# An AdaLN attention and mixture-of-experts layer on one core: where the zero rows are written, and how the first block's q, k and v are made

## The chip, the cores and the metric

The kernel runs on one core of a Trainium2 chip. The metric is the device time of one execution in microseconds, median of the runs. A core has five engines that run side by side, each its own list of instructions in order: TensorE (PE; its weight loads are PEld), VectorE (DVE), ScalarE (ACT), GpSimd (POOL) and SyncE (SP). Here SP issues nearly all transfers, ACT some, and POOL the indirect ones. Sixteen DMA engines carry out what the queues issue. [...]

## The reference

One layer of a diffusion transformer on x of shape 4 x 2048 x 256 in float32: a modulated LayerNorm, causal attention with 16 heads of size 16 and rotary positions, a gated residual, a second modulated LayerNorm, and a mixture of 16 experts (4 chosen of each token) with a shared expert. Cut to what matters here:

```python
mod = (silu(c) @ wmod).reshape(4, 6, 1, 256)
sa, ca, ga, sb, cb, gb = six parts of mod
h = layernorm(x) * (1 + ca) + sa
q, k, v = split(h @ qkv_w + qkv_b)            # 16 heads of 16
q, k = rotary(q), rotary(k)
attn = softmax(mask(q @ k.T / 4)) @ v
x = x + ga * (attn @ out_w + out_b)
h = layernorm(x) * (1 + cb) + sb
tidx, tw = route(h)                           # 4 of 16 experts for a token
y = sum over the chosen experts of tw * (silu(h @ w1.T) * (h @ w3.T)) @ w2.T
x = x + gb * (y + shared expert(h))
```

## The kernel before

**Blocks.** The 8192 tokens are 16 blocks of 512 (`BT`), four to a batch row; a block is four tiles of 128 tokens. The kernel has a start (constants and the modulation), an attention part (up to about 2430 us in the profile) and an expert part.

**The start.** Constants are loaded through SP. Then a pool named `zero` is opened: DVE fills a tile `zeros` of 128 x 2 x 272 (L203, L204; the four columns that name experts get -1), and ACT issues 32 writes of it (L207), one for each of 16 experts in each of two phases, to the DRAM arrays `xs`. They set the first 256 rows of each expert's region. Tokens are scattered into `xs` later by POOL (L489), and those rows stand in front of an expert's own. The pool is closed, and the pools of the modulation are opened in the memory that it gave back: `wm` (1.5 MB, L233), `sg` (L235), the matmuls on them (L240, L253), two gates on DVE, and a write of the result to DRAM (`rowd`, L265). When these are closed in turn, the attention's constants (`wqkv`, `bqkv`, `rp` and others) go into memory that they used.

**A prologue for each block** (`prologue`): load x (`xb`, L657), normalise on DVE and POOL, transpose with PE (L303), scale and shift on ACT into `hT` (L664). Then, for each tile `t` in turn: q and k as one matmul group of 512 columns into a PSUM tile `pq` (L698), bias on DVE (`qk`, L702); v into `pv` (L711), bias on DVE into `va` (L714); two products with the rotary table on POOL (L725) and their sum on POOL (L734); four transpositions of 128 x 128 into `ptq` (L739); and on ACT a copy rounded to the matmul's short float32 form (`high`, L748) and an exact copy (`whole`, L750). POOL subtracts one from the other (`low`, L678, function `lower`). `pq`, `pv`, `ptq` and the transposed x all share the one buffer of PSUM pool `wps`, so each waits until the one before has been read.

`high` and `low` hold two tiles and have one buffer. After the second and the fourth tile `store` writes them to DRAM (`qd`, `kd`) in 16 transfers of 8 heads x 16 x 256 (L689), 128 KB each; the third tile's `high` must wait until these have been read. v goes to `vd` (L756). The stores are for the next stage, in which a unit loads its heads (`load`): `qt` (L775), `kt` (L782) and `vg` (L785), with three buffers each.

**Units.** A unit is one group of four heads of one block of the first batch row, or of two blocks of a later one. `row_max` computes scores (L803, L826) only to find the row maxima on DVE (L813, L836); then the scores are computed again with the maxima subtracted (L1055, L1062), exponentiated on ACT (L1070), masked on POOL (L1074) and multiplied with v (L1003). The maxima of the next unit are found between the steps of the current one. PSUM pool `psp` has three buffers of two banks for scores, `pop` one bank for sums.

**Order.** Within the attention and expert parts PE, ACT, DVE and POOL run in the order in which the code is written. The transfers on SP are put in order by a planner. Before the first unit the code drains `prologue(0)` and the first unit's maxima; all other prologues, the ends of blocks and the routing are generators, pulled in pieces between the steps of the units. A piece states its need (a bank, DVE time, POOL time) and takes it from a `Budget` that each step refills, which can run into debt; due times (`due`) force a prologue's pieces in any case. `PIECES` is the number of pieces that `prologue(0)` had, and sets the due times.

Of the kernel before, what the change touches and what calls it, by code (L numbers as in the profile page):

```python
# [8 lines left out]
F32 = mybir.dt.float32  # L9
FR = mybir.dt.float32r  # L10
# [4 lines left out]
ALU = mybir.AluOpType  # L15
AX = mybir.AxisListType

P = 128
B, T, D = 4, 2048, 256
H, HD = 16, 16  # L20
NG = 4
BT = 512
HB = BT // 2
NQ = T // BT
NB = B * NQ
E, I = 16, 192
EW = 2 * 2 * I + 2 * D
N = B * T
TT = 256
TC = TT // P  # L30
# [5 lines left out]
ROW = D + 4 + 4 + 8  # L36
# [84 lines left out]
def adaln_attention_moe(  # L121
# [17 lines left out]
    nc = tc.nc  # L139
# [3 lines left out]
    const = ctx.enter_context(tc.tile_pool(name="const", bufs=1))  # L143
# [3 lines left out]
    ident = const.tile([P, P], F32, name="ident")  # L147
# [29 lines left out]
    phases = [Phase(blocks) for blocks in PHASES]  # L177
# [20 lines left out]
    nc.gpsimd.iota(  # L198
        four, [[4 * P, 4]], base=-1, channel_multiplier=4, allow_small_or_imprecise_dtypes=True
    )  # L200
    with tc.tile_pool(name="zero", bufs=1) as zp:
        zeros = zp.tile([P, TC, ROW], F32, name="zeros")
        nc.vector.memset(zeros, 0.0)  # L203
        nc.vector.memset(zeros[:, :, D : D + 4], -1.0)  # L204
        for ph in phases:
            for e in range(E):
                nc.scalar.dma_start(  # L207
                    ph.xs[e * ph.region : e * ph.region + TT, :].rearrange(
                        "(p t) d -> p (t d)", p=P
                    ),  # L210
                    zeros.rearrange("p t d -> p (t d)"),
                )

    mod = const.tile([P, 4, B], F32, name="mod")
# [12 lines left out]
    with tc.tile_pool(name="modw", bufs=1) as mw, tc.tile_pool(  # L229
        name="modp", bufs=1, space=PSUM  # L230
# [7 lines left out]
        for m in range(4):  # L238
            for k in range(2):
                nc.tensor.matmul(  # L240
                    pm[:, m, :],
                    lhsT=wm[:, k, m * P : (m + 1) * P],
                    rhs=sg[:, k, :],
                    start=(k == 0),
                    stop=(k == 1),
# [4 lines left out]
        for m in range(4):  # L250
            pr = mp.tile([B, D], F32, name=f"pr{m}")
            for k in range(2):
                nc.tensor.matmul(  # L253
                    pr,
                    lhsT=sg[:, k, :],
                    rhs=wm[:, k, (2 + m) * D : (3 + m) * D],
                    start=(k == 0),
                    stop=(k == 1),
# [336 lines left out]
    vd = [dram.tile([P, NG, 4, VG], F32, name=f"vd{n}") for n in range(NB)]  # L595

    with ExitStack() as actx:
# [3 lines left out]
        tp = actx.enter_context(tc.tile_pool(name="ta", bufs=2))  # L601
        ep = actx.enter_context(tc.tile_pool(name="ea", bufs=4))

        psp = actx.enter_context(tc.tile_pool(name="ps", bufs=3, space=PSUM))
        pop = actx.enter_context(tc.tile_pool(name="po", bufs=1, space=PSUM))
        wps = actx.enter_context(tc.tile_pool(name="wps", bufs=1, space=PSUM))
# [15 lines left out]
        wqkv = acst.tile([P, 2, 3 * D], F32, name="wqkv")  # L622
        nc.sync.dma_start(wqkv, qkv_w.rearrange("(k p) n -> p k n", p=P))
        bqkv = acst.tile([P, 3 * D], F32, name="bqkv")
# [5 lines left out]
        rp = acst.tile([P, T // P, 2, 2, HD // 2], F32, name="rp")  # L630
# [15 lines left out]
        va_new = acst.tile([P, NG, 4, VG], F32, name="va")  # L646
        vh = va_new[:, :, :, : 4 * (HD + 1)].rearrange("p g t (h e) -> p g t h e", e=HD + 1)
# [4 lines left out]
        def prologue(n):  # L652

            b, qb = divmod(n, NQ)
            yield 0, 0, 0
            xb = xp.tile([P, 4, D], F32, tag="xp", name="xb")
            nc.sync.dma_start(xb, x[n * BT : (n + 1) * BT, :].rearrange("(t p) d -> p t d", p=P))  # L657
            for _ in range(3):
                yield 0, 0, 0
            xn = yield from normalise(xb, tp, xb)  # L660
            yield 1, 0, 0

            def evict(to, pt, k):
                nc.scalar.activation(  # L664
                    to,
                    pt,
                    AF.Identity,
                    bias=mod[:, k, b : b + 1],
                    scale=mod[:, 2 + k, b : b + 1],
                )  # L670

            hT = yield from transposed(xn, "hT", tp, wps, "w", evict)


            rest = None

            def lower(cols, whole, high, low):
                nc.gpsimd.tensor_tensor(  # L678
                    low[:, :, cols], whole, high[:, :, cols].bitcast(F32), ALU.subtract
                )  # L680

            def store(half, high, low):

                for c_ in range(4):
                    to = (qd, kd)[c_ // 2][n].rearrange("(h part d) t -> part h d t", part=4, d=HD)
                    to = to[:, 8 * (c_ % 2) : 8 * (c_ % 2) + 8]
                    for part in range(4):
                        of = (high, low, *((high, low) if c_ < 2 else (low, high)))[part]
                        nc.sync.dma_start(  # L689
                            to[part][:, :, half * HB : (half + 1) * HB], of[:, c_, :].bitcast(F32)  # L690
                        )

            for t in range(4):
                lT = [hT[:, k, t * P : (t + 1) * P] for k in range(2)]
                yield 1, 0.7, 0
                pq = wps.tile([P, BT], F32, tag="w", name="pq")
                for k in range(2):
                    nc.tensor.matmul(  # L698
                        pq, lhsT=lT[k], rhs=wqkv[:, k, : 2 * D], start=(k == 0), stop=(k == 1)
                    )  # L700
                qk = tp.tile([P, 2 * D], F32, tag="qk", name="qk", bufs=1)
                nc.vector.tensor_add(qk, pq, bqkv[:, : 2 * D])  # L702
                yield 0, 0, 1.3 if rest is not None else 0
                if rest is not None:
                    lower(*rest)
                    if t == 2:
                        store(0, *rest[2:])
                yield 1, 0.4, 0
                pv = wps.tile([P, D], F32, tag="w", name="pv")
                for k in range(2):  # L710
                    nc.tensor.matmul(  # L711
                        pv, lhsT=lT[k], rhs=wqkv[:, k, 2 * D :], start=(k == 0), stop=(k == 1)
                    )
                nc.vector.tensor_add(  # L714
                    vh[:, :, t, :, 1:],
                    pv.rearrange("p (g h e) -> p g h e", g=NG, e=HD),
                    bqkv[:, 2 * D :].rearrange("p (g h e) -> p g h e", g=NG, e=HD),
                )
                parts = qk.rearrange("p (h e two) -> p h e two", e=HD // 2, two=2)
                full = [P, 2 * H, 2, HD // 2]  # L720
                prod = []
                for s in range(2):
                    yield 0, 0, 1.3
                    r_ = tp.tile(full, F32, tag=f"r{s}", name=f"r{s}", bufs=1)
                    nc.gpsimd.tensor_tensor(  # L725
                        r_,
                        parts[:, :, :, s].unsqueeze(2).to_broadcast(full),
                        rp[:, qb * 4 + t, s].unsqueeze(1).to_broadcast(full),
                        ALU.mult,
                    )  # L730
                    prod.append(r_.rearrange("p h a e -> p h (a e)"))
                xr = prod[0]
                yield 0, 0, 1.3
                nc.gpsimd.tensor_tensor(xr, xr, prod[1], ALU.add)  # L734
                yield 0, 0, 0
                yield 1, 0, 0
                pt = wps.tile([P, 4, P], F32, tag="w", name="ptq")
                for c_ in range(4):
                    nc.tensor.transpose(  # L739
                        pt[:, c_, :],  # L740
                        xr[:, 8 * c_ : 8 * c_ + 8, :].rearrange("p h d -> p (h d)"),
                        ident,
                    )
                if t % 2 == 0:
                    high = tp.tile([P, 4, HB], FR, tag="high", name="high", bufs=1)
                    low = tp.tile([P, 4, HB], FR, tag="low", name="low", bufs=1)
                cols = slice(t % 2 * P, (t % 2 + 1) * P)
                nc.scalar.copy(high[:, :, cols], pt)  # L748
                whole = tp.tile([P, 4, P], F32, tag="whole", name="whole", bufs=1)
                nc.scalar.copy(whole, pt)  # L750
                rest = (cols, whole, high, low)
            yield 0, 0, 1.3
            lower(*rest)
            yield 0, 0, 0
            store(1, *rest[2:])
            nc.sync.dma_start(vd[n], va_new)  # L756

        qts, kts, vas = {}, {}, {}


# [196 lines left out]
        ahead, maxes, after_max, over, ends, after = (Background(budget) for _ in range(6))  # L957
        ahead.add(prologue(0))
        ahead.drain()
        PIECES = ahead.pulled  # L960
        ahead.pulled = 0
        load(0)
        load(1)
        maxes.add(row_max(*units[0][0]))
        maxes.drain()
        after_max.drain()
        for n in range(1, NQ):
            ahead.add(prologue(n))
        for n in range(NQ, NB, NQ):
# [49 lines left out]
        for u, unit in enumerate(units):  # L1019
# [22 lines left out]
            for s_, (n, g, k_, nkt, off) in enumerate(steps_):  # L1042
# [9 lines left out]
                for q in range(2):  # L1052
                    for h_ in range(2):
# [3 lines left out]
                            start=True, stop=False,  # L1057
                        )
                for q in range(2):
                    for h_ in range(2):  # L1060
# [3 lines left out]
                            lhsT=kt[rows, q, k_ * P : (k_ + 1) * P],  # L1064
# [437 lines left out]
```

## Time and profile before

| | us |
|---|---|
| median of 3 runs | 3942.05 (3936.0 to 3945.19) |
| the profiled execution's own time | 3947.4 |
| its span | 3945.6 |
| `zeros` written, first issue to last landing | 1.84 to 31.7 |
| `wm` issued; first matmul on it | 31.68; 38.50 |
| `hT` of block 0 complete | 64.3 |
| first score matmul | 129.66 |
| first scatter into `xs` | 572.7 |
| PE, DVE, ACT, POOL busy | 3315.9, 2583.1, 1525.7, 1531.1 |

Times within an execution count from the start of its span. The span runs from the first instruction to the last; the execution's own time is 1.8 us more. The clock in a window's row is the granted clock of TensorE as a share of the full one, and the DMA share is the mean busy share of the sixteen DMA engines.

### The profile page before, as it was taken

How to read it: one execution, taken by the hardware profiler on the slowest of the kernel's cores; microseconds unless marked ns; L12 is line 12 of the kernel's file. 1: busy time of each engine (PE TensorE's matmuls, PEld its weight loads, DVE VectorE, ACT ScalarE, POOL GpSimd, SP SyncE). 2: the span in 40 equal slices, each digit the busy share in tenths (PEclk: the TensorE clock that was granted, in tenths of full speed). 3: DMA queues.
4: the chain of work that ended last, by engine and by line, in shares of the span. 5: the costliest groups of instructions: out<-in, count | busy, mean ns of one | idle time of the engine just before them, and what ended most of it. 6: DMA issues, size and time to landing. Idle time of an engine off the chain costs nothing. (4 is left out here: it accounts for less than half of the span.)

```text
span 3945.6 us, 56494 instructions
## 1 busy us (share of the span) xinstructions
PE 3315.9 (84%) x20276; PEld 1727.9 (44%) x20400; DVE 2583.1 (65%) x4644; ACT 1525.7 (39%) x2188; POOL 1531.1 (39%) x2222
## 2 busy tenths in 40 slices
PE   3567888888888989988898888899788889899994
PEld 1223333333334433333433333343377677676662
DVE  1344676767776777767767776677276576667775
ACT  0223344544444544544454454455522222222220
POOL 1223243352434342343425334310146556545555
PEclk7668898988999988988999998899999899899997
DMA  4233233341223322233332222220177567678763
GB/s 168 91 101 115 84 128 112 121 147 54 85 96 125 116 94 91 82 108 117 108 110 100 83 99 81 96 73 28 59 272 243 199 231 250 217 270 303 275 252 139
DMA packets 275115, 544.96 MB, mean 138 GB/s; under 512 B 27534, under 2 KB 143246, under 8 KB 274834
## 3 DMA queue, kind: packets, MB, share of 16 engines
q1 hardware_dynamic: 242578, 454.79, 33.9%
q0 software_dynamic: 27648, 77.63, 5.3%
q10 hardware_dynamic: 4608, 8.91, 0.6%
q8 instruction: 161, 2.64, 0.3%
q14 instruction: 120, 0.98, 0.1%
HBM read 351.42 MB, written 189.81 MB: 137 GB/s over the span
## 5 line engine op out<-in xcount | busy, mean ns | idle before, releaser
L1070 ACT ACTIVATE e<-st 128x1024 f32<-128x1024 f32 (+3 forms) x1280 | 1078.8, 895 | 1039.5 <-PE st L1062 960.3
L813 DVE TENSOR_REDUCE mparts<-ps 128x2 f32<-128x1024 f32 (+3 forms) x1152 | 1180.0, 1044 | 457.1 <-PE ps L803 409.4
L803 PE MATMUL ps<-kt,qt 64*128 64x512 f32 (+3 forms) x3328 | 613.6, 414 | 177.9 <-ACT e L1070 66.7
L1003 PE MATMUL po<-e,vg 128*32 128x512 f32 (+3 forms) x5120 | 670.6, 590 | 29.5 <-POOL e L1074 14.8
L803 PEld LDWEIGHTS ps<-kt,qt 64*128 64x128 f32 x3328 | 303.3, 203 | 769.3 <-ACT e L1070 447.3
L1074 POOL TENSOR_SCALAR_AFFINE_SELECT e<-e 128x256 f32<-128x256 f32 x512 | 204.7, 410 | 952.2 <-ACT e L1070 948.1
L1171 PE MATMUL gu<-xT,wt 128*128 128x256 f32 x1920 | 465.4, 397 | 24.1 <-issue 11.4
L1274 POOL DMA_INDIRECT yd<-yt,to x320 | 315.8, 987 | 390.7 <-ACT hb L1182 208.3
L1062 PE MATMUL st<-qt,kt 64*128 64x512 f32 (+3 forms) x2560 | 462.3, 441 | 0.0
L1171 PEld LDWEIGHTS gu<-xT,wt 128*128 128x128 f32 x1920 | 371.3, 198 | 112.9 <-issue 45.5
L1055 PE MATMUL st<-mt,pick 32*128 32x512 bf16 (+3 forms) x2560 | 302.5, 373 | 79.7 <-DVE mparts L813 49.0
L489 POOL DMA_INDIRECT xs<-row,rowx x256 | 248.4, 970 | 177.7 <-DVE row L480 122.7
L836 DVE TENSOR_REDUCE mparts<-ps 128x8 f32<-128x1024 f32 x128 | 156.7, 1224 | 196.8 <-PE ps L803 181.8
L1062 PEld LDWEIGHTS st<-qt,kt 64*128 64x128 f32 x2560 | 206.2, 199 | 138.5 <-issue 126.7
L725 POOL TENSOR_TENSOR r<-qk,rp 128x512 f32<-128x512 f32 x128 | 164.8, 1306 | 189.3 <-DVE qk L702 185.7
L1270 ACT ACTIVATE yt<-y,of 128x256 f32<-128x256 f32 x160 | 67.1, 470 | 403.5 <-DVE is L1250 213.9
L1055 PEld LDWEIGHTS <-pick 32*128 32x128 bf16 x2560 | 87.4, 92 | 303.2 <-issue 291.1
L1003 PEld LDWEIGHTS po<-e,vg 128*32 128x32 f32 x5120 | 109.2, 112 | 186.9 <-issue 129.1
L678 POOL TENSOR_TENSOR low<-whole,high 128x512 fp32r<-128x512 f32 x64 | 81.4, 1271 | 253.7 <-ACT whole L750 253.7
L1209 PE MATMUL y<-wt,ha 128*128 128x256 f32 x640 | 158.6, 389 | 10.8 <-issue 7.7
L698 PE MATMUL pq<-wqkv,hT 128*128 128x512 f32 x256 | 145.1, 694 | 17.4 <-ACT whole L750 14.9
L1209 PEld LDWEIGHTS y<-wt,ha 128*128 128x128 f32 x640 | 118.6, 195 | 32.7 <-issue 14.7
(209 smaller groups left out, 3603.4 us busy)
## 6 DMA issues: line engine op xcount, KB each, us to landing
wt<-in_w_all SPq DMA_DIRECT2D x160, 640.0 KB
kt<-kd SPq DMA_DIRECT2D x124, 512.0 KB
xt<-xs SPq DMA_DIRECT2D x160, 272.0 KB
qt<-qd SPq DMA_DIRECT2D x64, 512.0 KB
yg<-yd SPq DMA_DIRECT2D x16, 2048.0 KB
vg<-vd SPq DMA_DIRECT2D x124, 168.0 KB
xb<-in_x SPq DMA_DIRECT2D x32, 512.0 KB
qd<-high SPq DMA_DIRECT2D x128, 128.0 KB
```

The costliest lines, as they stand in the source:

```text
L489: s_ = nc.gpsimd.indirect_dma_start(out=ph.xs[:, :], out_offset=bass.IndirectOffsetOnAxis(ap=rowx[:, n, t, j : j + 1], axis=0), in_=row[:, ...
L725: nc.gpsimd.tensor_tensor(r_, parts[:, :, :, s].unsqueeze(2).to_broadcast(full), rp[:, qb * 4 + t, s].unsqueeze(1).to_broadcast(full), ALU ...
L803: nc.tensor.matmul(ps[:, half, to : to + width], lhsT=qt[rows, q, t * P : (t + 1) * P], rhs=kt[rows, q, key : key + width], start=start, s ...
L813: nc.vector.tensor_reduce(to, ps[:, :, :width], AX.X, ALU.max)
L1003: nc.tensor.matmul(po[32 * j : 32 * j + 32, off:], lhsT=va[:, k_, j * (HD + 1) : j * (HD + 1) + 32], rhs=es[j // 2][:, j % 2, off:], start ...
L1055: nc.tensor.matmul(sts[q][:, h_, off:], lhsT=pick[rows, :], rhs=mt[rows, off:], start=True, stop=False,)
L1062: nc.tensor.matmul(sts[q][:, h_, off:], lhsT=kt[rows, q, k_ * P : (k_ + 1) * P], rhs=qt[rows, q, off:], start=False, stop=True,)
L1070: nc.scalar.activation(es[q][:, :, off:], sts[q][:, :, off:], AF.Exp, scale=SCALE)
L1074: nc.gpsimd.affine_select(out=es[q][:, :, off : off + P], in_=es[q][:, :, off : off + P], compare_op=ALU.is_ge, fill=0.0, base=0, pattern= ...
L1171: nc.tensor.matmul(ps[:, c_ * TT : (c_ + 1) * TT], lhsT=wt[:, c_, k * 2 * I + cols : k * 2 * I + cols + P], rhs=xT[:, k, c_ * TT : (c_ + 1 ...
L1209: nc.tensor.matmul(pss[half][:, t, :], lhsT=ha[:, at_ : at_ + P], rhs=wt[:, half, 4 * I : 4 * I + D], start=(t == 0), stop=False, skip_gro ...
L1274: s_ = nc.gpsimd.indirect_dma_start(out=ph.yd[:, :], out_offset=bass.IndirectOffsetOnAxis(ap=to[:, t : t + 1], axis=0), in_=yt[:, t, :], i ...
```

## The change

The zeros become a tile of 128 x 272 in the constants' memory. They are filled by POOL after the code of the first unit's maxima, and written from SP, with each row of the tile written twice:

```diff
-    with tc.tile_pool(name="zero", bufs=1) as zp:
-        zeros = zp.tile([P, TC, ROW], F32, name="zeros")
-        nc.vector.memset(zeros, 0.0)
-        nc.vector.memset(zeros[:, :, D : D + 4], -1.0)
-        for ph in phases:
-            for e in range(E):
-                nc.scalar.dma_start(
...
+    zeros = const.tile([P, ROW], F32, name="zeros")
...
         maxes.drain()
         after_max.drain()
+        nc.gpsimd.memset(zeros, 0.0)
+        nc.gpsimd.memset(zeros[:, D : D + 4], -1.0)
+        for ph in phases:
+            for e in range(E):
+                nc.sync.dma_start(
+                    ph.xs[e * ph.region : e * ph.region + TT, :].rearrange(
+                        "(p t) d -> p t d", p=P
+                    ),
+                    zeros.unsqueeze(1).to_broadcast([P, TC, ROW]),
+                )
```

Block 0 gets a function of its own, `opening`, instead of the loop over tiles. q, k and v of a tile go into one two-bank buffer of the score pool `psp`, which has three; the biased q and k go into buffers of the pool `ep` that the units use for exponentials. Of the two rotary products one is made on POOL and one on DVE, and the sum on DVE. Copies into `high` and `whole` are in a function `high_low`, which both paths use.

```diff
+            def opening(hT, high_low, store):
+                full = [P, 2 * H, 2, HD // 2]
+                qks, rots = {}, {}
+                def project(t):
+                    ps = psp.tile([P, 2, BT], F32, tag="s", name="first")
+                    for to, cols in ((ps[:, 0], slice(0, 2 * D)), (ps[:, 1, :D], slice(2 * D, 3 * D))):
+                        for k in range(2):
+                            nc.tensor.matmul(to, lhsT=hT[:, k, t * P : (t + 1) * P], rhs=wqkv[:, k, cols],
...
+                    qk = ep.tile([P, 2, BT], F32, tag="e", name="qk0")
+                    nc.vector.tensor_add(qk[:, 0], ps[:, 0], bqkv[:, : 2 * D])
+                    nc.vector.tensor_add(vh[:, :, t, :, 1:], ...
+                def rotate(t):
...
+                    for s, eng in enumerate((nc.gpsimd, nc.vector)):
+                        r_ = tp.tile(full, F32, tag=f"r{s}", name=f"r{s}", bufs=1)
+                        eng.tensor_tensor(r_, ..., ALU.mult)
...
+                    nc.vector.tensor_add(xr, prod[0], prod[1])
+                def split(t):
...
+                    cols, whole = high_low(t, pt)
+                    high, low = parts_[0]
+                    lower(cols, whole, high, low)
+                    if t % 2:
+                        store(t // 2, high, low)
+                project(0)
+                project(1)
+                rotate(0)
+                project(2)
+                for t in range(4):
+                    if t < 3:
+                        rotate(t + 1)
+                    if t == 0:
+                        project(3)
+                    split(t)
```

Block 0's stores go out on two queues, and its prologue ends after `opening`; `PIECES` becomes the number that it was before:

```diff
-                        nc.sync.dma_start(
+                        queue = nc.scalar if n == 0 and part % 2 else nc.sync
+                        queue.dma_start(
...
+            if n == 0:
+                opening(hT, high_low, store)
+                nc.sync.dma_start(vd[n], va_new)
+                return
...
+        PIECES = 48
...
         ahead.add(prologue(0))
         ahead.drain()
-        PIECES = ahead.pulled
```

More of the change, by code (lines that the diff above doesn't have):

```diff
@@ L200, in adaln_attention_moe @@
     )
-    with tc.tile_pool(name="zero", bufs=1) as zp:
-        zeros = zp.tile([P, TC, ROW], F32, name="zeros")
-        nc.vector.memset(zeros, 0.0)
-        nc.vector.memset(zeros[:, :, D : D + 4], -1.0)
-        for ph in phases:
-            for e in range(E):
[L207 to L212, printed above, removed]
+    zeros = const.tile([P, ROW], F32, name="zeros")
     mod = const.tile([P, 4, B], F32, name="mod")
@@ L675, in prologue, with high_low @@
             rest = None
+            parts_ = [None]
+            def high_low(t, pt):
+                if t % 2 == 0:
+                    parts_[0] = tuple(
+                        tp.tile([P, 4, HB], FR, tag=name, name=name, bufs=1)
+                        for name in ("high", "low")
+                    )
+                cols = slice(t % 2 * P, (t % 2 + 1) * P)
+                nc.scalar.copy(parts_[0][0][:, :, cols], pt)
+                whole = tp.tile([P, 4, P], F32, tag="whole", name="whole", bufs=1)
+                nc.scalar.copy(whole, pt)
+                return cols, whole
@@ new lines, in opening @@
+            def opening(hT, high_low, store):
[5 more added lines that the diff above has]
+                        for k in range(2):
+                            nc.tensor.matmul(
+                                to,
+                                lhsT=hT[:, k, t * P : (t + 1) * P],
+                                rhs=wqkv[:, k, cols],
+                                start=(k == 0),
+                                stop=(k == 1),
+                            )
+                    qk = ep.tile([P, 2, BT], F32, tag="e", name="qk0")
+                    nc.vector.tensor_add(qk[:, 0], ps[:, 0], bqkv[:, : 2 * D])
+                    nc.vector.tensor_add(
+                        vh[:, :, t, :, 1:],
+                        ps[:, 1, :D].rearrange("p (g h e) -> p g h e", g=NG, e=HD),
+                        bqkv[:, 2 * D :].rearrange("p (g h e) -> p g h e", g=NG, e=HD),
+                    )
+                    qks[t] = qk
+                def rotate(t):
+                    qk = qks.pop(t)
+                    parts = qk[:, 0].rearrange("p (h e two) -> p h e two", e=HD // 2, two=2)
+                    prod = []
+                    for s, eng in enumerate((nc.gpsimd, nc.vector)):
+                        r_ = tp.tile(full, F32, tag=f"r{s}", name=f"r{s}", bufs=1)
+                        eng.tensor_tensor(
+                            r_,
+                            parts[:, :, :, s].unsqueeze(2).to_broadcast(full),
+                            rp[:, t, s].unsqueeze(1).to_broadcast(full),
+                            ALU.mult,
+                        )
+                        prod.append(r_.rearrange("p h a e -> p h (a e)"))
+                    xr = qk[:, 1].rearrange("p (h d) -> p h d", d=HD)
+                    nc.vector.tensor_add(xr, prod[0], prod[1])
+                    rots[t] = xr
+                def split(t):
+                    xr = rots.pop(t)
+                    pt = wps.tile([P, 4, P], F32, tag="w", name="ptq")
+                    for c_ in range(4):
+                        nc.tensor.transpose(
+                            pt[:, c_, :],
+                            xr[:, 8 * c_ : 8 * c_ + 8, :].rearrange("p h d -> p (h d)"),
+                            ident,
+                        )
+                    cols, whole = high_low(t, pt)
[13 more added lines that the diff above has]
+                    split(t)
@@ L743, in prologue @@
                     )
[L744 to L750, printed above, removed]
+                cols, whole = high_low(t, pt)
+                high, low = parts_[0]
                 rest = (cols, whole, high, low)
@@ L966, in adaln_attention_moe @@
         after_max.drain()
+        nc.gpsimd.memset(zeros, 0.0)
[7 more added lines that the diff above has]
+                    zeros.unsqueeze(1).to_broadcast([P, TC, ROW]),
+                )
         for n in range(1, NQ):
```

## The prediction

> **What bounds the kernel now.** I read the page first, then the timeline of the first 190 us, then the waits of the SP queue there, then the clock and DMA share by window. The page says what kind of place the change touches: TensorE is busy 84% of the span and sets its pace, but the first fortieth (99 us) has PE at 3 tenths and DVE at 1. Nothing runs beside the first block there, so an idle microsecond is one of the span; what comes after has its engines' order written out and moves forward whole.
>
> ```profile
> span 3945.6 us, 56494 instructions
> PE   3567888888888989988898888899788889899994
> q10 hardware_dynamic: 4608, 8.91, 0.6%
> ```
>
> The timeline shows three pieces before the first score matmul at 129.66: modulation weights `wm`, waited for until 38.50; a part to hT complete, about 64.3; then q, k and v of block 0, stored and read back, 65.3 us. The first line is from the waits of the SP queue (us in total, times, longest); the others are timeline rows (start, length, what, and in brackets how long the engine had been idle and what released it).
>
> ```profile
> SPq L233 <- DMA xs<-zeros: 26.7, 3, 25.3
> 1.84 27.18 ACTq L207 DMA_DIRECT2D xs<-zeros  x32
> 3.16 0.62 SPq L657 DMA_DIRECT2D xb<-in_x  x1
> 31.68 0.37 SPq L233 DMA_DIRECT2D wm<-in_wmod  x1
> 38.50 3.54 PE L240 MATMUL pm<-sg,wm 128*128 128x4 f32 x16 [38.50 <-DMA wm<-in_wmod]
> ...
> 64.36 3.78 PE L698 MATMUL pq<-wqkv,hT 128*128 128x512 f32 x4 [0.87 <-ACT hT L664]
> 68.92 2.08 PE L711 MATMUL pv<-wqkv,hT 128*128 128x256 f32 x4 [0.78 <-DVE qk L702]
> 85.00 0.58 ACT L748 CAST high<-ptq 128x512 fp32r<-128x512 f32 x1 [9.87 <-PE ptq L739]
> 85.61 2.00 SPq L689 DMA_DIRECT2D qd<-high  x3
> 99.52 0.59 ACT L748 CAST high<-ptq 128x512 fp32r<-128x512 f32 x1 [13.44 <-DMA kd<-high]
> 105.27 1.13 PE L711 MATMUL pv<-wqkv,hT 128*128 128x256 f32 x4 [0.84 <-DVE qk L702]
> 110.47 0.58 ACT L748 CAST high<-ptq 128x512 fp32r<-128x512 f32 x1 [9.88 <-PE ptq L739]
> 129.66 1.65 PE L803 MATMUL ps<-kt,qt 64*128 64x128 f32 x12 [18.38 <-DMA kt<-kd]
> 161.72 1.33 PE L803 MATMUL ps<-kt,qt 64*128 64x128 f32 x10 [0.36 <-issue]
> ```
>
> `wm` waits for the zeros because its pool reuses their memory; the page's queue 10 carries those 8.91 MB. The windows (start:end, length, busy and count of five engines, clock, DMA share, GB/s) show who limits what:
>
> ```profile
> 20.00:31.00 11.00, 0.00 (x0) 0.00 (x0) 0.00 (x0) 0.00 (x0) 0.00 (x0) 1.00 1.01 367
> 65.00:66.00 1.00, 1.00 (x2) 0.34 (x1) 0.00 (x0) 0.00 (x0) 0.00 (x0) 0.50 0.93 327
> 88.00:98.00 10.00, 5.10 (x11) 2.22 (x9) 1.12 (x2) 0.00 (x0) 3.82 (x3) 0.50 0.53 181
> 142.00:156.00 14.00, 12.70 (x69) 5.45 (x68) 7.68 (x15) 4.49 (x6) 2.45 (x6) 0.50 0.00 1
> ```
>
> Zeros fill every DMA engine; the stores of q and k fill only half of them (0.53); and TensorE can be nearly busy and still have half its clock.
>
> **Part 1, the zeros leave the start.** In the order of instructions as the changed kernel is built, `wm` now stands sixth on SP, before the x loads, and waits for nothing. It goes out where x does today, 3.16, and needs its measured 38.50 - 31.68 = 6.82: PE starts at 10.0 instead of 38.5. If the two x loads behind it (1.05 MB at about 390 GB/s, 2.7 us) took all of their time from it, the gain would be 25.8; if nothing shares, 28.5. I take 28.3: they queue behind. The table load and `sg` on ACT (1.5 us), freed by the same wait, lie in `wm`'s flight. The removed DVE memsets (0.51 and 0.07) were hidden there too. The part to hT is unchanged and only moves.
>
> **Part 2, block 0.** Today's 65.3 us are: 21.2 from 64.36 to the second `high` complete (85.58); 13.9 until its stores have landed and `high` may be overwritten (99.52); 11.5 to the fourth `high` complete (111.05); 18.6 to the scores.
> - *Projections together.* All sixteen matmul groups now run before any transposition. A tile costs 3.78 + 2.08 = 5.9 at half clock and, by the rows at full clock (2.01 at 175.93 us, 1.13 at 105.27), 3.1. In the fourth tile today the clock rose after 3.78 us without a gap, in the first three it did not. With some 15 us without a gap I take one tile slow and three fast: 5.9 + 9.4 = 15.3. Bounds: 12.6 all fast, 23.4 all slow. Then transposition 0.66, `high` and `whole` 1.07, transposition 0.66, `high` 0.58, hand-overs 0.2: 3.2. So 18.5 for 21.2.
> - *Rotation.* One product of two goes from POOL (1.28 each) to DVE, with the sum; DVE's nearest row is the 128x512 bias addition, 0.69, bounds 0.4 and 1.3. Four per tile, 2.5 us of DVE, under 3.1 us of PE: hidden. Uncovered it would be 1.4 us, on the last tile. The moved memset of `zeros` on POOL (128x1344 took 1.22, so 0.3) falls in POOL's wait for the first scores.
> - *Stores on two queues.* 32 stores; half now go out on ACT. An issue is 0.57 to 0.62 us, so eight instead of sixteen would save 5 us a half if issuing were the limit. The row 88 to 98 says that it is not: 0.53 of the engines, 181 GB/s, for 2.1 MB is 11.6 us, whichever queue feeds it. I take no gain. v's store and three loads of it now come earlier and share those engines: 3 x 168 KB, half on the busy eight, 1.4 us at 181 GB/s; I charge half: 14.6 for 13.9. On ACT the 8 x 0.6 us hold up only the third `high`, which waits for these stores anyway.
> - The Trainium skill, "DMA: Bandwidth & Descriptors", sections "Issuing engines are not separate DMA queues" and "Why a DMA increments its semaphore by 16 and not by 1", says that a second queue saves issue time alone, and that the outermost size caps the engines used; 8 is the outer size of these stores. The trace agrees: 0.53. By issue alone the sum would be 10 us better.
> - *Second half.* Its projections are done, so it is `high`, `whole`, a cold transposition (1.12), `high`: 2.9 for 11.5.
> - *Tail.* The stores of 2.1 MB, halves of both units' q and unit 0's k (0.79 MB) on the busy half, 2.9 MB at 185 GB/s is 15.6, plus 1.5 to start and about 1.2 to be seen: 18.3. The wait for a second queue's k stores may add; I take today's 18.6 (17 to 21).
>
> Sum: 18.5 + 14.6 + 2.9 + 18.6 = 54.6 for 65.3, a gain of 10.7 (about 2 with the slow clock, 15 at best).
>
> **Part 3, the zeros behind the first loads.** 32 writes, now of 1088-byte rows, stand on SP after unit 0's and 1's q and k; behind them are q and k of unit 2, then unit 3, v, and a later x. They are reached some 4 us before the first score (time T) and flow from about T + 0.5. Rows of 1 KB move at 181/0.53 = 341 to 327/0.93 = 352 GB/s, so 8.91 MB is 25.8 us; unit 2's megabyte takes 2.8 and about 1.2 to be seen: T + 30.3. Its first use today is 161.72, T + 32.1. So it just fits, by 2 us; I charge 0.5. If a packet cost as much as one of twice the size does now (0.6% of 16 x 3945.6 us over 4608 packets, 82 ns; 8704 packets, 44.6 us), the wait would be 17 us. PE waits in order there, so all of it would be on the path. The scatters into these rows start at 572.7 us: no wait there.
>
> **Part 4, the budget.** Block 0 runs up less debt in the background's budget, so between about 370 and 480 us a few groups of block 1 to 3's work swap places. No work is added. Waits of PE for POOL's rotation (up to 3.3 us) are what such a swap moves; two of them bound it at 6 either way, I take 0.
>
> Together -28.3 - 10.7 + 0.5 = -38.5. The profiled execution took 3947.4 (span 3945.6), so 3908.9 for it; it stands 5.35 above the median, hence **3903.5** on the median's basis.
>
> **Rivals.**
> 1. *Clock stays at half.* 142 to 156 speaks for it: 12.70 of 14 us busy, clock 0.50. Against it: those matmuls use 32 or 64 rows, while dense ones raised the clock at 105. Projections 23.4, transpositions 0.9 slower: total -29.5, 3912.5. The Trainium skill, "TensorE: Matmul & The Clock Gate", section "What's actually happening", has the clock released after about 3.4 us of sustained work; the row 142 to 156 does not follow it. Chance 0.16.
> 2. *Zeros collide with unit 2's k.* 17 us of wait as priced above: 3920. For it: packets are halved, the margin is 2 us. Against it: 1 KB rows of x and of q show full rate. Chance 0.11.
> 3. *Slower.* The zeros are confined to few DMA engines, as the q and k stores are to half. Unit 2's k then lands at T + 4.5 + drain, the wait is drain - 27.6; it eats the whole gain at a drain of 66 us and shows as slower from 74 us, under 120 GB/s. On four engines (86 GB/s, 103 us) +37: 3979. For it: a row on 8 engines is in this very trace. Against: the outer size is 128 or 256 here, not 8, and the zeros of today, 128 partitions wide, fill 1.01. Chance 0.04.
> 4. *The first wait only changes its holder* (another reader of the same memory keeps `wm` back): 3931. The built order shows no wait at all. Chance 0.04.
>
> **How the numbers follow.** My forecast has 0.65. About 0.2%, 8 us, is what a measurement tells from no change. The range reaches from the best opening (15) with a good swap, 3889, to the collision, 3921; outside lie rivals 3 and 4 and the tails of the swap. Slower by over 8 us: 0.04, rival 3. Within 8 us: 0.03, part of rival 4 and a half-size rival 3. Faster: 0.93.
>
> **What would show it.** `wm` issued near 3 us and PE's first matmul near 10; hT complete near 36; four projections in 12 to 23 us with the clock rising; DMA share still about 0.53 during the stores and some 14 us between the second and third `high`; the first score near 91; the zeros at share 1 for about 26 us behind it, and no wait of PE for `kt` at unit 2 over 3 us. A share near 0.5 or less for the zeros would make the forecast wrong, or a wait for k about 31 us after the first score.

## The result, and the profile after

| | before | changed | ratio, 95% interval |
|---|---|---|---|
| median of 7 runs each, us | 3939.49 (3925.55 to 3947.16) | 3903.77 (3894.79 to 3913.82) | 0.9911 (0.9889 to 0.9934) |
| profiled execution: own time; span | 3947.4; 3945.6 | 3907.39; 3905.7 | |

The changed kernel is faster by 35.7 us of the medians, 0.9%, with an interval that ends below 1, and by 40.0 us of the profiled executions; 38.5 was forecast. The page first: the first fortieth of the span has PE at 3 tenths as before and DVE at 2 instead of 1, and queue 10, which carried the 8.91 MB of zeros, carries only the 2.1 MB of block 0's stores that ACT issues.

```profile
span 3905.7 us, 56489 instructions
PE   3677988979889889888888988899888888899994
q10 hardware_dynamic: 2176, 2.10, 0.2%
```

The timeline of the changed kernel (start, length, what, in brackets the engine's idle time and what released it) has the same stations as before, each at its new line number.

```profile
3.15 0.43 SPq L221 DMA_DIRECT2D wm<-in_wmod  x1
3.62 0.47 SPq L645 DMA_DIRECT2D xb<-in_x  x1
4.13 0.56 SPq L996 DMA_DIRECT2D xb<-in_x  x1
11.92 3.54 PE L228 MATMUL pm<-sg,wm 128*128 128x4 f32 x16 [11.92 <-DMA wm<-in_wmod]
...
36.76 12.22 PE L689 MATMUL first<-wqkv,hT 128*128 128x512 f32 x32
37.01 0.78 ACT L652 ACTIVATE hT<-pt,mod 128x512 f32<-128x512 f32 x1 [1.21 <-PE pt L291]
51.28 0.58 ACT L674 CAST high<-ptq 128x512 fp32r<-128x512 f32 x1 [0.75 <-PE ptq L726]
54.39 4.22 ACTq L762 DMA_DIRECT2D qd<-low  x4
67.24 0.59 ACT L674 CAST high<-ptq 128x512 fp32r<-128x512 f32 x1 [14.75 <-DMA vg<-vd]
69.52 0.58 ACT L674 CAST high<-ptq 128x512 fp32r<-128x512 f32 x1 [1.21 <-PE ptq L726]
85.59 26.67 SPq L1045 DMA_DIRECT2D xs<-zeros  x32
90.46 1.65 PE L878 MATMUL ps<-kt,qt 64*128 64x128 f32 x12 [20.55 <-DMA kt<-kd]
122.59 1.33 PE L878 MATMUL ps<-kt,qt 64*128 64x128 f32 x10 [0.36 <-issue]
```

Read downwards: `wm` waits for nothing and is used at 11.92 (38.50 before); `hT` is complete at 37.79 (64.3); the second `high` at 51.86; the third starts at 67.24, when the stores have been read out (the row names the loads of v, which were queued among these stores); the fourth is complete at 70.10; the first score is at 90.46 (129.66). Unit 2 starts 32.13 us later, 32.06 before, released by nothing but the instruction ahead of it: in this profile the zeros, issued from 85.59 on, cost it nothing. The windows of the changed kernel (start:end, length, busy and count of PE, PEld, DVE, ACT, POOL, then clock, DMA share, GB/s) answer to those shown of before:

```profile
36.00:40.00 4.00, 4.00 (x8) 2.06 (x9) 0.00 (x0) 0.78 (x1) 0.00 (x0) 0.50 0.38 131
40.00:44.00 4.00, 4.00 (x14) 2.51 (x13) 1.16 (x3) 0.00 (x0) 1.31 (x1) 0.97 0.00 0
44.00:49.00 5.00, 5.00 (x18) 2.98 (x17) 4.63 (x8) 0.00 (x0) 1.31 (x1) 1.00 0.00 2
54.00:64.00 10.00, 1.09 (x4) 0.72 (x4) 2.29 (x3) 0.00 (x0) 2.17 (x2) 0.50 0.56 174
71.00:81.00 10.00, 0.00 (x0) 0.00 (x0) 0.00 (x0) 0.00 (x0) 1.30 (x3) 0.50 0.58 178
90.00:113.00 23.00, 16.57 (x87) 8.52 (x88) 11.78 (x20) 5.32 (x6) 1.63 (x4) 0.50 1.12 351
```

The projections have half the clock for about 4 us and the full one after that; both sets of stores still use little more than half of the DMA engines; the zeros use all of them, at 351 GB/s beside the first units.

The shift of 39.2 us at the first score is there to the end: the last q and k projection of block 15 is at 2385.4 instead of 2425.1, the shared expert's last matmul at 3855.1 instead of 3895.2. In between it was 47.0 at the first scatter (525.7 for 572.7), where background work has changed places, and 44.1 at the first expert matmul (2815.7 for 2859.8); neither stays.

### The profile page after: what moved, and what is told of

It is laid out like the page before. It is cut to its first block, busy times and chain, and to the rows that moved or that the text cites. A ratio compares the mean times of both kernels' runs of the same rounds, so it can differ in the third digit from the quotient of the medians.

```text
span 3905.7 us, 56489 instructions
## 1 busy us (share of the span) xinstructions
PE 3298.8 (84%) x20276; PEld 1723.2 (44%) x20400; DVE 2585.4 (66%) x4650; ACT 1525.6 (39%) x2188; POOL 1522.0 (39%) x2216
## 5 line engine op out<-in xcount | busy, mean ns | idle before, releaser
L1087 PE MATMUL po<-e,vg 128*32 128x512 f32 (+3 forms) x5120 | 667.8, 588 | 27.4 <-POOL e L1158 15.7
L1255 PE MATMUL gu<-xT,wt 128*128 128x256 f32 x1920 | 462.9, 396 | 20.4 <-issue 9.5
L803 POOL TENSOR_TENSOR r<-qk,rp 128x512 f32<-128x512 f32 x120 | 154.4, 1305 | 168.4 <-DVE qk L780 164.8
L1293 PE MATMUL y<-wt,ha 128*128 128x256 f32 x640 | 161.7, 391 | 21.6 <-issue 18.5
L776 PE MATMUL pq<-wqkv,hT 128*128 128x512 f32 x240 | 128.3, 660 | 10.4 <-ACT whole L676 8.6
```

Of the source, the lines that this page charges most:

```text
L1087: nc.tensor.matmul(po[32 * j : 32 * j + 32, off:], lhsT=va[:, k_, j * (HD + 1) : j * (HD + 1) + 32], rhs=es[j // 2][:, j % 2, off:], start ...
L1255: nc.tensor.matmul(ps[:, c_ * TT : (c_ + 1) * TT], lhsT=wt[:, c_, k * 2 * I + cols : k * 2 * I + cols + P], rhs=xT[:, k, c_ * TT : (c_ + 1 ...
L1293: nc.tensor.matmul(pss[half][:, t, :], lhsT=ha[:, at_ : at_ + P], rhs=wt[:, half, 4 * I : 4 * I + D], start=(t == 0), stop=False, skip_gro ...
```

## The experiments

The two halves, the kernel with one queue, the shorter start and the changed kernel again were timed on a second chip, on which the kernel before took 3850 to 3854 us (two medians). The kernels with other zeros, and the shorter start at first, ran once, beside one run of the kernel before (3944 to 3951 us, near the first chip's). T is the first score, U the first score of unit 2. The kernel before has a profile on the first chip alone, so a shift of T is always taken from its 129.66.

### The two halves of the change

The zeros alone: the changed kernel without `opening`, block 0 tile by tile on one queue.

```diff
-                        queue = nc.scalar if n == 0 and part % 2 else nc.sync
+                        queue = nc.sync
...
-            if n == 0:
-                opening(hT, high_low, store)
-                nc.sync.dma_start(vd[n], va_new)
-                return
```

> Only the zeros move; block 0 is made tile by tile and stored from SP as before. If the two parts add up (theory), the first matmul on wm stands near 11.9 us, the first score near 103.1 (129.66 - 26.6) and unit 2's first scores 32 us later without a wait for its k; the time is about 26.6 us under the kernel before, ratio 0.993. If the early wm is worth less without the quick opening because something else is then late (rival), the first score stands later than 106.

The opening alone: the changed kernel with the zeros made by DVE and written by ACT at the start again.

```diff
-    zeros = const.tile([P, ROW], F32, name="zeros")
+    with tc.tile_pool(name="zero", bufs=1) as zp:
+        zeros = zp.tile([P, TC, ROW], F32, name="zeros")
...
+                nc.scalar.dma_start(
...
-        nc.gpsimd.memset(zeros, 0.0)
...
-                nc.sync.dma_start(
```

> Only block 0's opening changes; the zeros are written from ACT at the start as before. Theory: first matmul on wm at 38.5 as before, first score 12.6 us earlier than before, near 117, and the time 12.6 us under it, ratio 0.997. Rival: the second queue is ACT's, which has just written the zeros, and the gain is lost there: first score near 129.

The first line is the timeline of the zeros alone, the second that of the opening alone.

```profile
103.52 1.65 PE L874 MATMUL ps<-kt,qt 64*128 64x128 f32 x12 [18.35 <-DMA kt<-kd]
```

```profile
116.45 1.65 PE L889 MATMUL ps<-kt,qt 64*128 64x128 f32 x12 [19.84 <-DMA kt<-kd]
```

Against the 129.66 of before they gain 26.1 and 13.2 us at the first score, together 39.3; the change gained 39.2. So up to there the two parts add, and do not touch each other. Behind it one expectation failed: with the zeros alone unit 2 waited 2.06 us for its k (the section on the prediction comes back to this). Their times said less: ratios 0.9952 (0.9931 to 0.9973) and 0.9986 (0.9967 to 1.0004), about 18 and 5 us. They were therefore taken again beside the changed kernel.

> The changed kernel as it is, beside the three that follow on one chip, so that the four can be compared. By its first measurement: ratio 0.991 to the kernel before, first score near 90.5.

> The zeros moved, block 0 tile by tile as before, a second time and beside the changed kernel. At the first score the two halves of the change added up (26.1 + 13.2 of 39.2 us), in the times they did not clearly (about 17 and 5 of 31 to 36). Theory: what stands at the first score is carried to the end, and the times of the first measurement were off by their scatter of 10 us; then this kernel is 24 to 28 us under the kernel before and 11 to 15 above the changed one. Rival: part of each half's gain is lost later in the units; then it is again 14 to 20 under the kernel before.

> The opening of block 0 new, the zeros at the start as before, a second time and beside the changed kernel. Theory (carried to the end): 11 to 15 us under the kernel before, 24 to 28 above the changed one. Rival (lost later): 3 to 7 us under the kernel before.

| | T | time (runs) | ratio, interval | gain |
|---|---|---|---|---|
| changed | 91.86 | 3828.1 (5) | 0.9918 (0.9889 to 0.9947) | 25.5 |
| zeros alone | 103.98 | 3833.79 (6) | 0.9952 (0.9928 to 0.9976) | 19.8 |
| opening alone | 114.92 | 3846.7 (10) | 0.9967 (0.9946 to 0.9988) | 6.9 |

The gains are differences of medians; the ratios are taken otherwise and give 31.6, 18.5 and 12.7. The halves add either way: 19.8 + 6.9 = 26.7 for 25.5, and 31.2 for 31.6. All three medians gain less than T moved (37.8, 25.7 and 14.7), on the rival's side, though each of the three intervals holds the shift of T. The other four timings of this chip lie on the same side, so that all seven fall short of T's shift by 6 to 14 us, and in three the shift is just outside the interval (13.2 against 12.7 at most for the opening alone at first, 40.7 against 40.4 with one queue, 60.0 against 57.8 with the shorter start). That speaks for a part that is given back on this chip; as the shift is taken from a profile of the first chip, it is not settled. In the two profiles of the first chip nothing is given back: from U to the end it is 3783.9 us in the kernel before and 3783.1 in the changed one. In the seven profiles of the second chip this remainder lies between 3680.7 (zeros alone, first profile) and 3711.0 (changed); the two kernels that were profiled twice there differ by 10 (zeros alone, 3690.6 the next time) and 3 us. Runs of one kernel scatter by 20 to 30 us (3842.29 to 3864.09 in 16 of the kernel before). A gain of 5 us is not to be read from such times; at T, where profiles of kernels that are alike up to there lie within 3 us, it is.

### One queue for block 0's stores

```diff
-                        queue = nc.scalar if n == 0 and part % 2 else nc.sync
+                        queue = nc.sync
```

> The changed kernel with all of block 0's stores issued from SP. Theory: the stores are held by the half of the DMA engines that they use, at a share near 0.55, so the first score stays within 2 us of 90.5 and the time is the changed kernel's. Rival: issuing 16 instead of 8 transfers on one queue costs 0.6 us each, 5 us a half; first score near 100.

Timeline of this kernel:

```profile
51.73 0.59 ACT L674 CAST high<-ptq 128x512 fp32r<-128x512 f32 x1 [0.75 <-PE ptq L726]
68.55 0.59 ACT L674 CAST high<-ptq 128x512 fp32r<-128x512 f32 x1 [15.60 <-DMA vg<-vd]
70.82 0.59 ACT L674 CAST high<-ptq 128x512 fp32r<-128x512 f32 x1 [1.20 <-PE ptq L726]
88.97 1.65 PE L878 MATMUL ps<-kt,qt 64*128 64x128 f32 x12 [17.76 <-DMA kt<-kd]
```

From the end of the second `high` to the third it is 16.2 us, 0.8 longer than with two queues; from the end of the fourth to the first score 17.6, 2.8 shorter (20.4). T is 1.5 us earlier, within what kernels with two queues scatter (88.85 to 91.86 in the six profiles that are alike up to T), and the time is the same: ratio 0.9921 (0.9895 to 0.9946), 0.9918 with two queues. The second queue buys nothing.

### What if few DMA engines carried the zeros

This is the rival of the prediction by which the kernel would have become slower. Four kernels write the same 8.91 MB in rows of 1088 bytes at the same place in the program, in other shapes. Two long transfers of outermost size 16, and four of outermost size 8 (with 8 in place of 16):

```diff
-            for e in range(E):
+            for e in range(0, E, 16):
                 nc.sync.dma_start(
-                    ph.xs[e * ph.region : e * ph.region + TT, :].rearrange(
-                        "(p t) d -> p t d", p=P
+                    ph.xs.rearrange("(e r) d -> e r d", e=E)[e : e + 16, :TT, :].rearrange(
+                        "e (p t) d -> e p t d", p=P // 16
                     ),
-                    zeros.unsqueeze(1).to_broadcast([P, TC, ROW]),
+                    zeros.unsqueeze(1).to_broadcast([P, 16 * TT // P, ROW]),
```

> The changed kernel with the zeros written in two transfers (one for each phase) in place of 32, so that the outermost size of a transfer is 16 (experts) and a descriptor's row is the same 1088 bytes. A control for the next kernel. Both theories: all sixteen DMA engines, DMA share about 1.1 and 350 GB/s while the zeros go out, 25 to 28 us for them; first score near 90.5 as in the changed kernel; first score of unit 2 about 32 us behind it, without a wait for kt above 1 us.

> The same zeros, bytes and rows in four transfers of outermost size 8. Theory (the prediction's rival that ended slower: the outermost size sets how many DMA engines carry a transfer): share about 0.53 to 0.58 and 175 to 190 GB/s while the zeros go out, 8.91 MB in 47 to 51 us; the k of unit 2 stands behind them and lands about 51 us behind the first score, so PE waits there for kt some 18 to 22 us; everything later moves back by as much. Rival (it is the partitions or the row size, not the outermost size, that held the q and k stores to half of the engines): share 1.1, drain 26 us, no wait, as in the kernel with outermost size 16.

And the 32 transfers kept, read from 16 partitions or from 8 (with 8 in place of 16):

```diff
-                        "(p t) d -> p t d", p=P
+                        "(p t) d -> p t d", p=16
                     ),
-                    zeros.unsqueeze(1).to_broadcast([P, TC, ROW]),
+                    zeros[:16].unsqueeze(1).to_broadcast([16, TT // 16, ROW]),
```

> The changed kernel with its 32 transfers of zeros as they are, one for each expert, but each read from 16 partitions with a row written 16 times (in the changed kernel 128 partitions, twice), so that the outermost size is 16. Bytes, rows of 1088 bytes, order and destination are the same. Theory A (the outermost size alone sets how many DMA engines carry a transfer): share near 1.1, 350 GB/s, drain 26 us, no wait for kt at unit 2, everything as in the changed kernel. Theory B (in the two kernels with the long transfers, each DMA engine wrote into the region of one expert, or read from few partitions, and that made its rows dearer: 0.94 of the engines for 215 GB/s): if few partitions are the reason, the same is seen here, share about 0.94, 215 to 260 GB/s, drain 34 to 41 us and a wait of 8 to 16 us; if it is the regions, nothing of it is seen here.

> The same with 8 partitions, a row written 32 times, outermost size 8. Theory A: half of the DMA engines, share 0.53 to 0.58, 175 to 185 GB/s, drain 48 to 51 us, unit 2 waits for kt 20 to 25 us. Against it (the engines are filled by bytes and not by the outermost size): share above 0.9 and a drain like that of the run with 16 partitions. The wait is 26 to 31 us if the rows are dearer too (131 GB/s at the start, as in the long transfers of outermost size 8).

A window and the first score of unit 2 of each, in this order: long transfers of outermost size 16; of 8; from 16 partitions; from 8.

```profile
90.00:125.00 35.00, 21.45 (x134) 10.59 (x134) 16.98 (x37) 9.59 (x13) 5.04 (x11) 0.65 0.95 230
```

```profile
136.61 1.33 PE L878 MATMUL ps<-kt,qt 64*128 64x128 f32 x10 [18.12 <-DMA kt<-kd]
```

```profile
89.00:140.00 51.00, 23.79 (x134) 11.42 (x136) 16.80 (x37) 9.59 (x13) 5.10 (x11) 0.53 0.54 162
```

```profile
150.06 1.33 PE L878 MATMUL ps<-kt,qt 64*128 64x128 f32 x10 [30.48 <-DMA kt<-kd]
```

```profile
95.00:180.00 85.00, 21.85 (x122) 9.82 (x120) 14.49 (x34) 9.58 (x13) 5.08 (x11) 0.52 0.84 93
192.13 1.33 PE L878 MATMUL ps<-kt,qt 64*128 64x128 f32 x10 [69.64 <-DMA kt<-kd]
```

```profile
100.00:250.00 150.00, 18.83 (x106) 8.05 (x106) 10.38 (x28) 9.58 (x13) 5.08 (x11) 0.52 0.43 48
281.21 1.33 PE L878 MATMUL ps<-kt,qt 64*128 64x128 f32 x10 [159.03 <-DMA kt<-kd]
```

| zeros written | share, GB/s | 8.91 MB at that rate | less 27.6 | unit 2 late | time, before |
|---|---|---|---|---|---|
| changed kernel | 1.12, 351 | 25.4 | none | 0 | 3903.77, 3939.49 |
| two long, outermost 16 | 0.95, 230 | 38.7 | 11.1 | 14.8 | 3931.41, 3950.53 |
| four long, outermost 8 | 0.54, 162 | 55.0 | 27.4 | 29.1 | 3926.65, 3950.53 |
| 32, from 16 partitions | 0.84, 93 | 95.8 | 68.2 | 68.5 | 3966.83, 3944.12 |
| 32, from 8 partitions | 0.43, 48 | 185.6 | 158.0 | 157.8 | 4065.18, 3944.12 |

"Late" is U - T less the 32.1 of the changed kernel. The prediction's rule for the wait, the drain less 27.6, holds within 4 us over the whole range. The point from which the change is slower, put at a drain of 66 to 74 us, was only bracketed: at 55.0 the kernel is still 23.9 us faster, at 95.8 it is 22.7 us slower, and at 185.6 it is 121 us slower (-38.5 + 157.8 = 119 by the rule), each in its one run. From U to the end these four take 3793.1, 3774.8, 3773.0 and 3782.2 us, within 10 of the 3783.1 of the changed kernel: as far as that tells, nothing of the wait is made up later.

Outermost size 8 does halve the engines: 0.43 for 0.84, 0.54 for 0.95. The long transfers of outermost size 8 were slower than expected, though (162 GB/s for 175 to 190, a wait of 30.5 us for 18 to 22), and the expectation of the controls failed. With outermost size 16 the engines are filled and still move 230 and 93 GB/s, not 350; what the second theory put at 215 to 260 GB/s for 16 partitions was 93. How the zeros are spread over partitions matters as much as how many engines carry them.

### A shorter start

In the changed kernel SP waits longest, in its first 40 us, for the modulation's rows (this is its view of SP's waits: total, times, longest):

```profile
SPq L253 <- DVE rows L215: 18.7, 1, 18.7
...
SPq L611 <- DMA rowd<-rows: 1.4, 1, 1.4
```

`rowd` at 23.45 and `wqkv` at 25.34 stand behind it, though block 0 needs neither the rows nor their gates. The edit loads c, x, `wm` and `wqkv` in this order, takes `wm` into a buffer that `kt` uses later, makes the rows between the second and third transposition of block 0, loads the expert part's constants behind block 0, and leaves one queue:

```diff
+        nc.sync.dma_start(cT, c)
+        nc.sync.dma_start(first_x, x[:BT, :].rearrange("(t p) d -> p t d", p=P))
+        wm = kvp.tile([P, 2, T], FR, tag="kt", name="wm")[:, :, : 6 * D].bitcast(F32)
+        nc.sync.dma_start(wm, wmod.rearrange("(k p) n -> p k n", p=P))
+        wqkv = acst.tile([P, 2, 3 * D], F32, name="wqkv")
+        nc.sync.dma_start(wqkv, qkv_w.rearrange("(k p) n -> p k n", p=P))
...
             xn = yield from normalise(xb, tp, xb)
+            if n == 0:
+                modulation()
...
                     split(t)
+                    if t == 1:
+                        modulation_rows()
...
+        late_constants()
```

> The changed kernel with a shorter start: the loads are ordered by what is needed first (c, x of block 0, wm, wqkv and its bias), x of block 0 is normalised while wm is in flight, the four row vectors of the modulation and their gates (with the write of rowd) are made in the gap in which the first half's q and k are being stored, the constants of the expert part are loaded behind the first block, and block 0's stores all go out on SP. Theory: nothing but wm, x and wqkv is needed for block 0, and the part from wm's matmuls (12) to hT complete (38) is serial work of the rows, the gates and rowd. Then PE's first matmul on wm comes near 9, hT complete near 17 to 20, first score near 68 to 72 (90.5 in the changed kernel), and the time is 18 to 22 us under the changed kernel's. Rival: the part to hT is held by the DMA engines (wqkv, rp and x landing), then hT stays complete near 30 or later, and the gain is under 8 us.

> The kernel with the shorter start, timed. In its single look it had its first score at 70.0 and its span 16.3 us under the changed kernel's. Theory: 20 us under the changed kernel and 55 to 60 under the kernel before (ratio 0.985 to 0.986). It falls if the two intervals overlap with that of the changed kernel.

Timeline of its first run:

```profile
9.23 3.55 PE L580 MATMUL pm<-sg,wm 128*128 128x4 f32 x16 [9.23 <-DMA wm<-in_wmod]
...
15.95 12.69 PE L703 MATMUL first<-wqkv,hT 128*128 128x512 f32 x32
16.20 0.78 ACT L666 ACTIVATE hT<-pt,mod 128x512 f32<-128x512 f32 x1 [1.21 <-PE pt L255]
...
69.97 1.65 PE L894 MATMUL ps<-kt,qt 64*128 64x128 f32 x12 [18.49 <-DMA kt<-kd]
```

`hT` is complete at 16.98 instead of 37.79, and T falls by 20.5. Of these 21 us, 2.7 are `wm`, which now goes out right behind c and x, at 1.73 instead of 3.15, and is used at 9.23 instead of 11.92. The other 18 lie between its first matmul and `hT` (7.8 us for 25.9): the rows, the gates and `rowd`, and the normalisation and other work that stood behind them. The rival, that landing loads hold `hT` to near 30, fell. The first run took 3891.17 for 3950.53. Timed on the second chip, it took 3807.62 (3803.59 to 3814.82, 4 runs), ratio 0.9878 (0.985 to 0.9905): 46 us under the kernel before and 20.5 under the changed kernel beside it, where T moved by 22.2; 55 to 60 under the kernel before had been expected. The two ratio intervals overlap by 0.0016, so by its own criterion the times do not separate it from the changed kernel; the profiles do, at T.

## Why the prediction was right

The forecast was 3903.5 and the median is 3903.77. The path was right at each step: `wm` no longer waits, the stores are held by half of the engines, the zeros drain before unit 2 needs its k. Two of its reasons were not (that the loads queue behind `wm`, and which matmuls raise the clock), and the terms were off by up to 4.4 us in both directions:

| term | predicted | measured |
|---|---|---|
| PE's first matmul on `wm`, from 38.50 to | about 10 (gain 28.3) | 11.92 (26.6) |
| projections to second `high` complete | 18.5 | 14.1 |
| its stores, to third `high` | 14.6 | 15.4 |
| to fourth `high` complete | 2.9 | 2.9 |
| to the first score | 18.6 | 20.4 |
| block 0 in all | 54.6 (gain 10.7) | 52.7 (12.6) |
| zeros against unit 2's k | 0.5 | 0 |
| sum | -38.5 | -39.2 at T, -40.0 at the end |

That the sum comes so near is in part luck. Terms of 4.4 and 0.5 that were put too high stand against 1.7, 0.8 and 1.8 put too low. The median's 0.3 us is luck altogether: the medians differ by 35.7 and not 38.5, and the kernel before came out 2.6 us under the 3942.05 from which the forecast was reckoned. The lower end of the range, 3889, does not follow from its words either; the best opening and a swap of 6 us give about 3893.

- *Part 1.* "I take 28.3: they queue behind" was mis-sized. `wm` was in flight for 11.92 - 3.15 = 8.8 us instead of 6.82. The two x loads issued 0.5 and 1.0 us behind it took most of these 2.0 us: up to 12.00 the engines moved 2.46 MB, 0.7 MB more than `wm` and the constants ahead of it hold, which is 1.7 us at the 400 GB/s of these microseconds. So here loads issued within a microsecond of each other shared the engines; the first did not pass whole before the next.
- *Projections.* 11.2 us from `hT` to the last one's end instead of 15.3. In the changed kernel DVE's bias additions stand 2.58 us apart, at 41.28, 43.86, 46.44 and 49.02, so a tile at full clock costs 2.58, not the 3.1 that two separate rows add up to; that is 1.7 us over three tiles. The other 2.4 lie in the first tile, priced at 5.9 in half clock: its addition comes 3.5 us behind `hT`, because it began at 36.76, on the half of `hT` that was ready, and because the clock rose before it was through (0.88 from 40 to 41 us).
- *Clock.* The rival with 0.16 fell: the rows 36 to 49 show 0.50, then 0.97 and 1.00. In 90 to 113 PE is busy 16.57 of 23 us at 0.50, as at 142 to 156 before. The prediction told the two apart by the matmuls, dense ones of 128 rows against short ones of 32 or 64. These rows fit that, but as a rule it does not hold: with the opening alone the same short matmuls of unit 1 have clock 1.00 at the place where they have 0.50 in the changed kernel (rows below). What decides is open. The Trainium skill, "TensorE: Matmul & The Clock Gate", section "What's actually happening", has the clock released after about 3.4 us of sustained work; the rows from 36 on agree (4 us), that of 90 to 113 does not follow it.
- *Rotation* was hidden: the product on DVE took 0.68 to 0.83, and PE went from projections to transpositions without a gap (48.82).
- *Stores on two queues.* Right, shown by the kernel with one: the share stays near 0.5 either way (0.56 and 0.58 here, 0.47 and 0.53 there). The tail's excess of 1.8 us lies with the second queue, as the prediction's bound of 21 allowed: with it the tail took 19.4 to 21.0 in all eight profiles, with one queue 17.6 to 19.0 in the five of other kernels and 18.6 before.
- *Zeros.* 25.4 us of drain for 25.8 predicted, unit 2 at T + 32.13 for T + 32.1; how narrow that was stands below. The rival of dearer packets (17 us of wait) fell; the long transfers, at 230 GB/s, show what it would have done (14.8). The slower rival was worth its place: its mechanism and its rule are real, and of the five shapes that ran only this one, 128 partitions with a row written twice, kept it away.
- *Budget.* Worth nothing in the end, as taken: the shift is 39.2 at the first score, 47.0 at the first scatter and 39.7 at block 15.
- *The first wait only changes its holder* fell at 3.15.

The clock, 25 to 30 us behind T, with the opening alone (second profile) and in the changed kernel:

```profile
139.92:144.92 5.00, 4.18 (x51) 2.33 (x48) 3.39 (x14) 3.16 (x6) 2.96 (x6) 1.00 0.67 205
```

```profile
115.46:120.46 5.00, 4.33 (x32) 1.45 (x32) 3.19 (x14) 2.17 (x5) 2.64 (x5) 0.50 0.75 256
```

That the zeros cost unit 2 nothing hangs in part on this clock. In both profiles of the changed kernel unit 1 ran at 0.50, and PE reached unit 2 at T + 32.1 without a wait. In all five other profiles with the zeros in this shape PE waited there for `kt`: 2.06 and 4.78 us with the zeros alone, 3.02 with one queue, 3.63 and 0.44 with the shorter start. With the opening alone, where no zeros stand ahead of that load, the clock rose and unit 2 came at T + 28.96 and T + 29.07. The first scores of unit 2, with the opening alone (T 114.92) and with one queue (T 88.97), where the clock rose too:

```profile
143.99 0.81 PE L889 MATMUL ps<-kt,qt 64*128 64x128 f32 x10
```

```profile
121.16 1.33 PE L878 MATMUL ps<-kt,qt 64*128 64x128 f32 x10 [3.02 <-DMA kt<-kd]
```

In the three profiles with the zeros in which the clock rose ahead of unit 2 (waits of 3.02, 3.63 and 4.78) it came at T + 32.2 to T + 33.6, 3 to 4.6 us later than with the opening alone. So the margin was as thin as the prediction said, or thinner: both profiles of the changed kernel kept it with TensorE at half clock, two others at half clock (waits of 2.06 and 0.44) did not, and where the clock rose it was gone. No run had the changed kernel itself with the clock risen there.

## What to carry to other kernels

Where nothing runs beside the first block, price each microsecond there in full, and look for what holds the first load or the first matmul: here memory reused from a pool, and rows that nobody needed yet. Work moved behind the critical loads is free only as long as its drain is shorter than the time to the next load's first use, so work out that margin (here 27.6 us for 25.4, which was not enough where TensorE ran faster) and what spreads the transfer over engines and partitions. Judge a gain of 10 us in a run of 3900 at the place where it arises, since runs of one kernel scatter by 20 to 30.

## What the runs showed of the hardware that was not expected

Filled engines are not a full rate. Reading from 16 partitions the DMA engines are 0.84 busy at 93 GB/s, from 8 partitions 0.43 busy at 48: 5.8 and 6.0 GB/s an engine, where the changed kernel has 351/16 = 21.9. That an engine reads one partition row after row doesn't explain it alone: in the long transfers of outermost size 16, if an engine has one expert there, as the layout suggests, it writes each of eight partitions' rows 32 times in turn, and still at 216/16 = 13.5 GB/s (row below, 100 to 112 us of that kernel).

```profile
100.00:112.00 12.00, 10.18 (x53) 4.60 (x54) 4.57 (x6) 5.32 (x6) 1.63 (x4) 0.51 0.94 216
```

The Trainium skill, "SBUF — State Buffer", section "Door 1: The DMA port swizzle", puts partitions 0 to 15 on four of sixteen ports and 0 to 7 on two. The traces agree so far: 93/4 = 23 and 48/2 = 24 GB/s a port, the same in both. No run read the same number of partitions spread over more ports, and in these two kernels an engine also writes longer runs of DRAM (16 or 32 rows in a row instead of two), so that the ports are the reason is not shown.
